# Values spread over a head's partitions: 0/1 products on TensorE, or rows read eight times from HBM

## The chip, the cores and the metric

The kernel runs on one core of a Trainium2 chip. The metric is the device time of one execution in microseconds (us), given as the median of several runs. The core's engines are TensorE (PE, matrix products, with its weight loads listed as PEld), VectorE (DVE), ScalarE (ACT), GpSimd (POOL) and SyncE (SP, which here issues nearly all DMAs). SBUF is the on-chip memory of 128 partitions, PSUM the memory into which TensorE writes its products, HBM the memory off the core.

## The reference

Everything is float32. `x` has 32 batches of 64 tokens of 256 features, and `ctx_2048` the same shape; four blocks follow each other on `x`:

- layer 0: self-attention, cross-attention into `ctx_2048` (16 heads of 16), a GELU MLP;
- layer 1: a recurrent block (32 heads of 8) and a gated feed-forward part;
- layer 2: two cross-attentions (16 heads of 128, with one bias key and value each) and a GELU MLP;
- layer 3: a cross-attention (16 heads of 16) and a GELU MLP.

The change lies in layer 1's recurrence. For each batch and head it keeps an 8×8 state `s`, and for each of the 64 tokens:

```python
def step(s, rkvw):
    r_t, k_t, v_t, w_t = rkvw
    a = k_t[..., :, None] * v_t[..., None, :]
    out = jnp.einsum('bhi,bhij->bhj', r_t, u * a + s)
    s = a + w_t[..., :, None] * s
    return (s, out)
```

So column j of a head's state takes the eight values of k, each times the one value j of v: value j of each head is needed beside all eight of that head's k.

## The kernel before

The 2048 tokens are worked in four groups of 512 (8 batches each, `G`, `GT`, `GB`), and the 256 features lie on partitions in two chunks `c` of 128 (`NC`), so that a chunk holds 16 heads of 8 features. A layer of a group is a Python generator that yields between steps, and `weave(main, lights)` takes steps of the generators in turn at fixed rates:

- layer 0 of group 0, beside `keep`, a filler that makes layer 2's first keys and values (`fk`, `fv`) and stores them in HBM (`kd`, `vd`);
- layer 1 of group 0, beside layer 0 of group 1 and the filler;
- layer 2 of group 0 beside layer 1 of group 1 and layer 0 of group 2; layer 2 of group 1 beside layer 1 of group 2 and layer 0 of group 3; layer 2 of group 2 beside layer 1 of group 3 and layer 3 of group 0;
- then the remaining layers 2 and 3.

So layer 1 of group 0 is the main stream of its stage, while those of groups 1 to 3 are the lighter stream beside the attention of layer 2 (L748 on: products `q2p`, `s2p`, softmax, `pn` on POOL, transposes `tp`, products `pv`, DVE's `o`, then `al_o` through L328). From the order of this program text the scheduler of the framework makes one fixed instruction order per engine; each engine works in order and waits on semaphores.

Tiles come from rotating pools. `banks()` gives one of two double PSUM banks (128×2×512), `bank()` one of four single ones, `big()` one of the 12 SBUF tiles "t4" of 128×2×512. `slot()` loads a 512 KB weight block by a DMA from SP's queue.

In layer 1 (`layer1`, L440), r, k and v of a group are made by `linear` (L165) with the features as partitions, and copied to SBUF by ACT (L521). `ws` holds the decays. `states(c, n)` (L542) makes two of the eight columns j of chunk c's states, n = 0 to 3:

- two products with a 0/1 matrix (L550; columns `C_SEL` of the constants `ct`) take the 32 rows of v that hold value j of the 16 heads, and put each head's row on that head's eight partitions, in the PSUM tile `vj`. The features are laid out so that the 16 rows 16·j to 16·j+15 of a chunk are value j of its 16 heads, and the partitions 8·h to 8·h+7 of the state are head h;
- POOL copies the initial state into column 0 of each batch of `a` (L555);
- DVE multiplies `vj` by k into the remaining columns of `a`, one token later (L559);
- DVE runs the recurrence along the tokens, a scan for each of the two columns (L565);
- POOL multiplies by r (L566).

PE then sums over each head's partitions (`op`, L588). Two states are made ahead; the loop (from L578) makes state n+2 and then consumes state n. After four states of a chunk, `bp` (L595) and two DVE operations on v (L596, L597) complete it, and group norm, gate and output product follow (`gm` L603, `gv` L609).

The helper `beside(i)` raises the priority of the second of two products so that it is placed right behind the first, on other rows of the array.

Of the kernel before, what the change touches and what calls it, by code (L numbers as in the profile page):

```python
# [8 lines left out]
F32 = mybir.dt.float32  # L9
# [5 lines left out]
P = 128  # L15
# [3 lines left out]
GT = NT // G  # L19
GB = B // G  # L20
TT = GT // P
NC = D // P
# [5 lines left out]
C_ID, C_HB, C_HB8, C_SEL, C_GAT, C_M0, C_M1 = 0, 128, 256, 384, 640, 704, 705  # L28
# [40 lines left out]
def kernel(  # L69
# [15 lines left out]
    nc = tc.nc  # L85
    V, A, PL, PE = nc.vector, nc.scalar, nc.gpsimd, nc.tensor
# [4 lines left out]
    sm = ctx.enter_context(tc.tile_pool(name="sm", bufs=2))  # L91
    psum1 = ctx.enter_context(tc.tile_pool(name="ps1", bufs=4, space=bass.MemoryType.PSUM))
    psum2 = ctx.enter_context(tc.tile_pool(name="ps2", bufs=2, space=bass.MemoryType.PSUM))

    def bank(name):
        return psum1.tile([P, 512], F32, tag="b1", name=name)

    def banks(name):
        return psum2.tile([P, 2, 512], F32, tag="b2", name=name)

    def slot(i, pool=lw):
        w = pool.tile([P, WSLOT], F32, tag="w", name=f"w{i}")
        nc.sync.dma_start(w, wts[i])
        return w
# [12 lines left out]
    ct = cp.tile([P, C_N], F32, name="ct")  # L117
# [43 lines left out]
    def linear(ps, w, at, step, y, cols=P):  # L161

        for kc in range(NC):
            o = at + kc * step
            PE.matmul(ps, w[:, o : o + cols], y[:, kc, :], start=(kc == 0), stop=(kc == NC - 1))  # L165
# [251 lines left out]
    @contextmanager  # L417
    def beside(i):

        if i:  # L420
            with tc.high_priority(offset=4000):
                yield
        else:
            yield

    def bt(ap):

        return ap.rearrange("p (b t) -> p b t", b=GB)
# [11 lines left out]
    def layer1(g, work):  # L440
# [3 lines left out]
        def big(name):  # L444
            return work.four(f"{name}_{g}")
# [21 lines left out]
        def mixed(*fs):  # L467

            xms = [big(f"xm{f}") for f in fs]
            parts = [(f, c) for c in range(NC) for f in fs]  # L470
            for two in (parts[:2], parts[2:]):
                if not two:
                    continue
                mp = banks(f"mp_{g}_{two[0][0]}{two[0][1]}")
                for i, (f, c) in enumerate(two):
                    at, rows = c * P, slice(32 * f, 32 * f + 32)
                    if f == 4:
                        at, rows = D + c * P, slice(32 * c, 32 * c + 32)
                    with beside(i):
                        PE.matmul(mp[:, i, :], w6[rows, at : at + P], t5[rows, f // 4, :], start=True, stop=True)  # L480
                for i, (f, c) in enumerate(two):
                    V.scalar_tensor_tensor(
                        xms[fs.index(f)][:, c, :], mp[:, i, :], vec("L1_xattn_maa_stack", 2 * f + c), sx[:, c, :],
                        ALU.add, ALU.mult,
                    )
            for xm in xms:
                PL.tensor_tensor(xm, xm, xa, ALU.add)
            return xms
# [18 lines left out]

        w7 = slot(L1_AT + 2)
        made = {}
        for f, n, at in ((0, "k", 0), (2, "v", 512)):  # L510
            if f == 0:
                xm = xk
            else:
                xm, xr = mixed(2, 3)
                yield
                yield
            made[n] = big(n)
            for c in range(NC):
                ps = bank(f"{n}p1_{g}_{c}")
                linear(ps, w7, at + c * P, D, xm)  # L520
                A.copy(made[n][:, c, :], ps)  # L521
            yield
        w8 = slot(L1_AT + 3)
        xm = xr
# [15 lines left out]
        k, v, r = made["k"], made["v"], made["r"]  # L540

        def states(c, n):  # L542

            j0 = (0, 4, 1, 5)[n]
            vj = banks(f"vj_{g}_{c}_{n}")
            for i in range(2):
                m, q = (j0 + 2 * i) // 2, j0 % 2
                rows = slice(32 * m, 32 * m + 32)
                with beside(i):
                    PE.matmul(  # L550
                        vj[:, i, :], ct[rows, C_SEL + q * P : C_SEL + (q + 1) * P], v[rows, c, :],
                        start=True, stop=True,
                    )
            a = big(f"a{c}{n}")
            PL.tensor_copy(  # L555
                a.rearrange("p i (b t) -> p i b t", b=GB)[:, :, :, 0:1],
                s0t[:, c, j0 : j0 + 3 : 2, g * GB : (g + 1) * GB].unsqueeze(3),
            )
            V.tensor_tensor(  # L559
                a.rearrange("p i (b t) -> p i b t", b=GB)[:, :, :, 1:],  # L560
                vj.rearrange("p i (b t) -> p i b t", b=GB)[:, :, :, :-1],
                bt(k[:, c, :])[:, :, :-1].unsqueeze(1).to_broadcast([P, 2, GB, S - 1]), ALU.mult,
            )
            for i in range(2):
                V.tensor_tensor_scan(a[:, i, :], ws[:, c, :], a[:, i, :], 0.0, ALU.mult, ALU.add)  # L565
            PL.tensor_tensor(a, a, r[:, c : c + 1, :].to_broadcast([P, 2, GT]), ALU.mult)  # L566
            return j0, a

        ruk = big("ruk")
        todo = [(c, n) for c in range(NC) for n in range(4)]  # L570
        ahead = [states(*todo[0])]
        yield
        ahead.append(states(*todo[1]))
        yield
        for c in range(NC):
            V.scalar_tensor_tensor(ruk[:, c, :], r[:, c, :], vec("L1_xattn_u", c), k[:, c, :], ALU.mult, ALU.mult)
        w9 = slot(L1_AT + 4)
        for at, (c, n) in enumerate(todo):  # L578
            if at + 2 < 8:
                ahead.append(states(*todo[at + 2]))  # L580
                yield
            if n == 0:
                op = bank(f"op_{g}_{c}")
            j0, a = ahead.pop(0)
            for i in range(2):
                m, q = (j0 + 2 * i) // 2, j0 % 2
                with beside(i):
                    PE.matmul(  # L588
                        op[32 * m : 32 * m + 32, :], ct[:, C_GAT + 32 * q : C_GAT + 32 * q + 32], a[:, i, :],
                        start=(q == 0), stop=(q == 1),  # L590
                    )
            yield
            if n == 3:
                bp = bank(f"bp_{g}_{c}")
                PE.matmul(bp, hb, ruk[:, c, :], start=True, stop=True)  # L595
                V.tensor_tensor(v[:, c, :], bp, v[:, c, :], ALU.mult)  # L596
                V.tensor_tensor(v[:, c, :], op, v[:, c, :], ALU.add)  # L597
                yield
# [311 lines left out]
            for _ in l[0]:  # L910
                pass

    dp = ctx.enter_context(tc.tile_pool(name="dp", bufs=1, space=bass.MemoryType.DRAM))
    kept = {}

    def keep(pool):
# [156 lines left out]
def build(arrays):  # L1073
    import concourse.bacc as bacc

    nc = bacc.Bacc("TRN2", target_bir_lowering=False, num_devices=1)
    args = [
        nc.dram_tensor(f"in_{n}", a.shape, mybir.dt.from_np(a.dtype), kind="ExternalInput").ap()
        for n, a in arrays.items()
    ]  # L1080
    args.append(nc.dram_tensor("out_0", (P, G, TT, D), F32, kind="ExternalOutput").ap())
    with tile.TileContext(nc) as tc:
        kernel(tc, *args)
    return nc
# [13 lines left out]
```

## Time and profile before

| | |
|---|---|
| runs (us) | 2219.75, 2216.74, 2218.61; median 2218.61 |
| profiled execution (us) | 2216.37, its span 2214.6 |
| granted TensorE clock, mean | 0.97 |
| instructions | 36273 |
| PE busy | 2057.4 us (93%) |
| DVE busy | 1097.3 us (50%) |
| ACT busy | 632.9 us (29%) |
| POOL busy | 597.5 us (27%) |
| DMA, all queues | 197.25 MB, mean 89 GB/s |
| layer 1's states, groups 0 to 3 | about 315 to 400, 583 to 645, 1018 to 1080, 1463 to 1526 us of the span |

The page is taken from one execution; the others can differ by a few tenths of a per cent. Busy time is the time in which an engine executes, not in which it is at its best rate. In a line for a group of instructions stand line, engine, operation, the tile written and the tiles read, the shape and the count, then durations in ns (smallest, median, largest) and first and last start. In a timeline line the bracket at the end gives the idle time before the entry and what released it. A window line gives its length, then the busy time and count of PE, PEld, DVE, ACT and POOL, the granted clock, the busy share of the DMA engines and GB/s.

### The profile page before, as it was taken

The page shows a single profiled execution, that of the slowest core. Times are in us where ns is not written, and L with a number is a line of the kernel's source. Part 1 is how long each engine was busy: PE and PEld are TensorE (multiplying, and loading weights), DVE is VectorE, ACT ScalarE, POOL GpSimd, SP SyncE. Part 2 cuts the span into 40 slices and gives each one's busy share as a digit, 9 for nine tenths or more (in the row PEclk, how much of TensorE's full clock was granted, in tenths as well). Part 3 has the DMA queues.
Part 4 walks back from the last instruction along what each step waited for, and adds up shares of the span by engine and source line. Part 5 has one row for each costly group of instructions (what it writes and reads, how often), then busy time and mean ns, then how long its engine had stood idle before and what let it go on. Part 6 is the DMA issues. An engine that isn't in the chain of part 4 may idle for free. (4 is left out here: it accounts for less than half of the span.)

```text
span 2214.6 us, 36273 instructions
## 1 busy us (share of the span) xinstructions
PE 2057.4 (93%) x15264; PEld 1242.9 (56%) x15264; DVE 1097.3 (50%) x1885; ACT 632.9 (29%) x1000; POOL 597.5 (27%) x498
## 2 busy tenths in 40 slices
PE   5889998899999898999997999999999999999998
PEld 3445444354555465755554656555566767565665
DVE  3552557423655636335556463266564355424661
ACT  1222322132321322232313132322233233222442
POOL 2331344213423314214324141233221112200220
PEclk9999998999999999999998999999999999999999
DMA  7233231226412212243121123341213342213010
GB/s 247 93 106 118 93 110 57 93 101 229 141 49 64 66 41 63 92 132 109 55 62 58 42 79 96 121 134 44 86 45 108 100 152 69 78 51 94 22 41 20
DMA packets 79794, 197.25 MB, mean 89 GB/s; under 512 B 9616, under 2 KB 14352, under 8 KB 79632
## 3 DMA queue, kind: packets, MB, share of 16 engines
q1 hardware_dynamic: 77472, 191.88, 27.1%
q8 instruction: 121, 1.98, 0.4%
q0 software_dynamic: 576, 2.10, 0.3%
q10 hardware_dynamic: 1584, 0.95, 0.2%
q14 instruction: 41, 0.34, 0.1%
HBM read 158.98 MB, written 35.91 MB: 88 GB/s over the span
## 5 line engine op out<-in xcount | busy, mean ns | idle before, releaser
L165 PE MATMUL q2p<-h,w 128*128 128x512 f32 x512 | 245.4, 612 | 6.8 <-DMA w<-in_wts 3.2
L328 PE MATMUL al_o<-w,o 128*128 128x256 f32 x1024 | 235.1, 388 | 11.7 <-DVE o L828 10.7
L328 PEld LDWEIGHTS al_o<-w,o 128*128 128x128 f32 x1024 | 196.6, 194 | 52.6 <-issue 20.6
L778 ACT ACTIVATE q<-q2p,vt 128x512 f32<-128x512 f32 x128 | 87.5, 685 | 278.9 <-PE q2p L165 275.7
L165 PEld LDWEIGHTS q2p<-h,w 128*128 128x128 f32 x512 | 94.9, 193 | 123.6 <-issue 105.5
L796 POOL TENSOR_TENSOR pn<-s,sm 128x512 f32<-128x512 f32 x64 | 69.7, 1091 | 285.2 <-DVE sm L209 198.2
L165 PE MATMUL k2p_f<-c,w 128*128 128x512 f32 x256 | 131.2, 634 | 4.9 <-DMA w<-in_wts 2.8
L726 PE MATMUL v2p_f<-w,c 128*128 128x512 f32 x256 | 122.4, 601 | 0.0
L165 PE MATMUL k2p<-c,w 128*128 128x512 f32 x256 | 120.7, 597 | 0.0
L726 PE MATMUL v2p<-w,c 128*128 128x512 f32 x256 | 119.1, 609 | 1.1 <-DVE k L764 1.1
L566 POOL TENSOR_TENSOR a<-a,r 128x1024 f32<-128x1024 f32 x32 | 76.1, 2378 | 109.8 <-DVE a L565 96.4
L937 DVE TENSOR_TENSOR fv<-v2p_f,vb 128x512 f32<-128x512 f32 x64 | 43.9, 687 | 124.7 <-PE v2p_f L726 124.7
L928 ACT ACTIVATE fk<-k2p_f,vt 128x512 f32<-128x512 f32 x64 | 43.9, 686 | 175.4 <-PE k2p_f L165 146.8
L341 DVE TENSOR_TENSOR x<-al_o,x 128x512 f32<-128x512 f32 x64 | 43.6, 683 | 101.2 <-PE al_o L328 101.2
L828 DVE TENSOR_SCALAR o<-pv,vt 128x256 f32<-128x256 f32 x128 | 55.8, 473 | 76.6 <-PE pv L817 76.4
L764 DVE TENSOR_SCALAR k<-k2p,vt 128x512 f32<-128x512 f32 x64 | 47.4, 743 | 91.4 <-PE k2p L165 91.4
L788 PEld LDWEIGHTS s2p<-k,q 128*64 128x64 f32 x2048 | 67.7, 138 | 40.8 <-issue 29.7
L817 PEld LDWEIGHTS pv<-pt,v 64*64 64x64 f32 x4096 | 72.8, 140 | 26.6 <-issue 18.4
L565 DVE TENSOR_TENSOR_SCAN a<-ws,a 128x512 f32<-128x512 f32 x64 | 85.4, 1368 | 1.7
L726 PEld LDWEIGHTS v2p_f<-w,c 128*128 128x128 f32 x256 | 49.6, 195 | 63.5 <-issue 61.3
L817 PE MATMUL pv<-pt,v 64*64 64x64 f32 x4096 | 81.7, 226 | 3.2 <-issue 1.5
L165 PEld LDWEIGHTS k2p<-c,w 128*128 128x128 f32 x256 | 49.4, 193 | 62.1 <-issue 59.4
(305 smaller groups left out, 3678.5 us busy)
## 6 DMA issues: line engine op xcount, KB each, us to landing
w<-in_wts SPq DMA_DIRECT2D x200, 512.0 KB, 3.7
kd<-fk SPq DMA_DIRECT2D x64, 260.0 KB, 2.1
k<-kd SPq DMA_DIRECT2D x64, 260.0 KB, 3.8
vd<-fv SPq DMA_DIRECT2D x64, 256.0 KB, 2.0
v<-vd SPq DMA_DIRECT2D x64, 256.0 KB, 4.5
vb<-in_vrow SPq DMA_DIRECT2D x20, 256.0 KB, 4.1
vs<-in_vrow SPq DMA_DIRECT2D x20, 256.0 KB, 3.4
c<-in_cT POOLq DMA_DIRECT2D x4, 512.0 KB, 11.6
```

Of the source, the lines that this page charges most:

```text
L165: PE.matmul(ps, w[:, o : o + cols], y[:, kc, :], start=(kc == 0), stop=(kc == NC - 1))
L328: PE.matmul(ps[:, a, :], y[kc][:, i * P : (i + 1) * P], wk[:, o : o + D], start=(kc == 0), stop=(kc == k - 1),)
L565: V.tensor_tensor_scan(a[:, i, :], ws[:, c, :], a[:, i, :], 0.0, ALU.mult, ALU.add)
L566: PL.tensor_tensor(a, a, r[:, c : c + 1, :].to_broadcast([P, 2, GT]), ALU.mult)
L726: PE.matmul(ps, cs[g][:, kc, bp * P : (bp + 1) * P], wv[:, 512 * kc : 512 * kc + 512], start=(kc == 0), stop=(kc == NC - 1),)
L764: V.tensor_scalar_add(k[:, :, :S], bt(ps), vec(f"L2_xattn_bk{a}", hd))
L778: A.activation(q, ps, AF.Identity, bias=vec(f"L2_xattn_bq{a}", hd))
L788: PE.matmul(sp[64 * h2 : 64 * h2 + 64, b // 4, (b % 4) * (S + 1) : (b % 4 + 1) * (S + 1)], qs[h2][:, b * S : (b + 1) * S], ks[h2][:, b, :] ...
L796: PL.tensor_tensor(pn, s[:, :, :S], rc.unsqueeze(2).to_broadcast([P, GB, S]), ALU.mult)
L817: PE.matmul(pv[b2][rows, to : to + S], vals[bp][half, hc : hc + 64], pt[half, bp, h2 * S : (h2 + 1) * S], start=True, stop=True,)
L828: V.tensor_scalar_add(ov[:, :, 1, :], src[1], bv)
L928: A.activation(k[:, :, :S], bt(ps), AF.Identity, bias=vec("L2_xattn_bk1", hd))
```

## The change

The two products of a state are left out, and with them the PSUM tile `vj`. Each chunk of v is stored to HBM as it is made (256 KB, `spread`). For each of a state's two columns a DMA then reads the column's 16 rows back, each eight times, and writes them to the 128 partitions of `a`, shifted by one token (255.5 KB). DVE's multiply reads `a` and writes it in place. The pool `dp` of HBM tensors is opened earlier, so that layer 1 can use it.

```diff
+    dp = ctx.enter_context(tc.tile_pool(name="dp", bufs=1, space=bass.MemoryType.DRAM))
...
         made = {}
+        spread = [dp.tile([P, GT], F32, name=f"vs{g}{c}", tag=f"vs{g}{c}") for c in range(NC)]
...
                 A.copy(made[n][:, c, :], ps)
+                if n == "v":
+                    nc.sync.dma_start(spread[c], made[n][:, c, :])
...
             j0 = (0, 4, 1, 5)[n]
-            vj = banks(f"vj_{g}_{c}_{n}")
+            a = big(f"a{c}{n}")
             for i in range(2):
-                m, q = (j0 + 2 * i) // 2, j0 % 2
-                rows = slice(32 * m, 32 * m + 32)
-                with beside(i):
-                    PE.matmul(
-                        vj[:, i, :], ct[rows, C_SEL + q * P : C_SEL + (q + 1) * P], v[rows, c, :],
-                        start=True, stop=True,
-                    )
-            a = big(f"a{c}{n}")
+                j = j0 + 2 * i
+                nc.sync.dma_start(
+                    a[:, i, 1:],
+                    spread[c][16 * j : 16 * j + 16, : GT - 1].unsqueeze(1).to_broadcast([16, 8, GT - 1]),
+                )
             PL.tensor_copy(
                 a.rearrange("p i (b t) -> p i b t", b=GB)[:, :, :, 0:1],
                 s0t[:, c, j0 : j0 + 3 : 2, g * GB : (g + 1) * GB].unsqueeze(3),
             )
             V.tensor_tensor(
                 a.rearrange("p i (b t) -> p i b t", b=GB)[:, :, :, 1:],
-                vj.rearrange("p i (b t) -> p i b t", b=GB)[:, :, :, :-1],
+                a.rearrange("p i (b t) -> p i b t", b=GB)[:, :, :, 1:],
                 bt(k[:, c, :])[:, :, :-1].unsqueeze(1).to_broadcast([P, 2, GB, S - 1]), ALU.mult,
             )
...
-    dp = ctx.enter_context(tc.tile_pool(name="dp", bufs=1, space=bass.MemoryType.DRAM))
     kept = {}
```

## The prediction

> **What bounds the kernel now.** I read the page's engine totals first, then the tile that the change removes, stage by stage, then the orders of PE, DVE and POOL around it, then the transfers.
>
> The totals:
>
> ```profile
> PE 2057.4 (93%) x15264; PEld 1242.9 (56%) x15264; DVE 1097.3 (50%) x1885; ACT 632.9 (29%) x1000; POOL 597.5 (27%) x498
> q1 hardware_dynamic: 77472, 191.88, 27.1%
> ```
>
> TensorE (PE) is busy for 93% of the span, and the DMA engines are idle for some 70%. So work taken off PE can shorten the kernel, but only where PE isn't waiting anyway. The removed tile `vj`, then PE's busy time on it in the four stages that hold it (groups 0 to 3), and last the same stages for the whole core (PE, PEld, DVE, ACT, POOL busy, then clock, DMA share, GB/s):
>
> ```profile
> L550 PE MATMUL vj<-v,ct x128: 587/692/1217, 316.4 to 1509.2; 32*128 32x512 f32 x128
> L559 DVE TENSOR_TENSOR a<-vj,k x32: 1177/1198/1209, 317.5 to 1509.9; 128x1008 f32<-128x1008 f32 x32
> 315.00:400.00 85.00, 9.97 (x32) 2.60 (x32) 9.50 (x8) 0.88 0.18 64
> 583.00:645.00 62.00, 7.90 (x32) 2.11 (x32) 9.57 (x8) 0.93 0.31 95
> 1018.00:1080.00 62.00, 7.90 (x32) 2.11 (x32) 9.58 (x8) 0.94 0.30 94
> 1463.00:1526.00 63.00, 8.18 (x32) 2.38 (x32) 9.59 (x8) 1.00 0.30 93
> 315.00:400.00 85.00, 69.08 (x377) 32.95 (x376) 67.36 (x71) 19.29 (x32) 41.96 (x28) 0.88 0.18 64
> 583.00:645.00 62.00, 54.96 (x481) 31.04 (x483) 42.68 (x49) 12.82 (x21) 25.12 (x15) 0.93 0.31 95
> 1463.00:1526.00 63.00, 60.92 (x690) 33.74 (x692) 46.68 (x58) 16.40 (x29) 25.79 (x16) 1.00 0.30 93
> ```
>
> The products cost PE 9.97 + 7.90 + 7.90 + 8.18 = 33.95 us, 1.06 us per tile of two (32 tiles). That is the ceiling, but for idle that goes with them. Group 0's stage is no PE stage: PE 69.1 of 85 us, DVE 67.4. Groups 1 and 2 leave PE idle for 7 of 62; group 3 for 2 of 63. What the products stand beside, group 1 then group 3 (start, length, idle before and its releaser):
>
> ```profile
> 596.81 1.13 PE L550 MATMUL vj<-v,ct 32*128 32x512 f32 x4
> 599.88 1.05 PE L588 MATMUL op<-a,ct 128*32 128x512 f32 x4 [0.84 <-POOL a L566]
> 602.89 1.10 PE L328 MATMUL al_o<-w,o 128*128 128x256 f32 x4 [0.90 <-PE vj L550]
> 607.17 8.57 PE L328 MATMUL al_o<-w,o 128*128 128x256 f32 x28 [3.18 <-DVE o L828]
> 641.52 1.05 PE L588 MATMUL op<-a,ct 128*32 128x512 f32 x4 [2.11 <-POOL a L566]
> ...
> 1469.67 6.28 PE L328 MATMUL al_o<-w,o 128*128 128x256 f32 x28 [0.72 <-DVE o L828]
> ```
>
> The 28 `al_o` products take 6.28 us in group 3 and 8.57 in group 1 behind the 3.18 us idle: an idle PE costs its length and about 2.3 us of slow clock.
>
> **What is removed.** 64 products (128 matmul and 128 weight-load rows), and DVE's wait for them.
>
> Group 0: 9.97 us leave PE, but DVE fills 79% of the stage and PE has its own waits there, the longest of 5.47 us for a DVE `fv` (L937) at 395.31, behind the last two scans (386.92, 7.75 us). In the changed order those scans come earlier, as chunk 1's third and fourth states do. Half of 9.97 is taken, 5, less the wait for `y_b` below, 2, plus 2 of the late idle: −5 (bounds −9 and +4).
>
> Groups 1 and 2, each: in the first half three tiles (3.2) come off a busy PE; the others stood in front of waits for the same DVE and POOL chain, but that chain no longer waits for PE (0.84 and 0.90 were such waits) and begins up to 3.6 us earlier, as the second multiply on `vj` moves ahead: −3.5 together. The three later tiles (620.28, 627.90, 631.02) stand among busy PE work: −3.2. The wait of 2.11 at 641.52 for POOL ends earlier, with the slow clock behind it: −2.3. With 1 back for DVE, below: −8 (bounds −10 and −4).
>
> Group 3: the first three tiles end just ahead of the wait for `o`. DVE, not PE, sets its end, and in the changed order one multiply (1.2 us) stands ahead of `o`, so these 3.2 us become idle. The five later ones give 5.3; 2.3 goes back if that idle turns the clock down. −3 (bounds −5.3 and +1).
>
> **What is added.** On SP's queue, 8 stores of 256 KB and 64 loads of 255.5 KB (128 rows of 2044 B), 72 DMAs and 18.8 MB on 197. The nearest rows, the last a row read 128 times:
>
> ```profile
> vd<-fv SPq DMA_DIRECT2D x64, 256.0 KB, 2.0
> v<-vd SPq DMA_DIRECT2D x64, 256.0 KB, 4.5
> vs<-in_vrow SPq DMA_DIRECT2D x20, 256.0 KB, 3.4
> 530.00:546.00 16.00, 12.21 (x57) 5.22 (x58) 5.34 (x9) 5.93 (x8) 2.07 (x2) 0.89 0.97 339
> ```
>
> A load lands in 3.4 to 4.5 us; I take 4, since the source is a tensor just written, as for `vd`. At 339 GB/s, which a full stretch reached, 18.8 MB are 55 us of transfer, in stages that use 18 to 31% of the DMA engines. The store's 2.0 is hidden: `r` and the gate's products come between it and the first state. Costed at nothing on SP: at the 0.32 to 0.43 us that it takes for an issue it has 23 to 31 us more to do, over 2215; its place in order matters more. In group 1 the loads stand behind a weight load that waits for `q2p` (578.5), so the first lands at about 583, before 584.33 where the first product stood. The fourth state's loads wait there for the first state's `op`, and eight `v` loads queue behind them, issued near 601 and not from 593; they are needed at 643, so 8 us of delay are covered by 40.
>
> Two waits are new. POOL's copy of column 0 (L555) now waits for the landing, since it writes the tile that the DMA fills, and all later POOL work is queued behind it in order. In group 0 the second state's copy stands behind an add that ends at 317.33; the scans on DVE then wait for it, and `y_b` (318.67) behind them starts some 2 us later, with PE's `qp_b` waiting. In group 1 the copy for the fifth state stands ahead of a `pn` multiply due at 592.54: a weight load and ten loads (3.07 MB) have 13.6 us to land, so 226 GB/s decides. In group 3 it is 2.05 MB in 9.5 us, 216 GB/s. At 339 both are covered.
>
> DVE's multiply (L559) now reads both inputs from SBUF. `L205`, two SBUF inputs of the same size, and the scan (also two):
>
> ```profile
> L205 DVE TENSOR_TENSOR s_b<-s_b,mx_b x16: 1182/1216/2756, 124.6 to 1299.4; 128x1024 f32<-128x1024 f32 x16
> L565 DVE TENSOR_TENSOR_SCAN a<-ws,a x64: 1160/1214/3294, 319.4 to 1512.7; 128x512 f32<-128x512 f32 x64
> ```
>
> Both have the median of L559 but a long tail that it lacks (their means are 1336 and 1368): +0.14 to 0.17 each, 4.5 to 5.5 us of DVE in all; no bound for PE but in group 0 and at the two waits for `o`, and counted there with 1 per stage.
>
> [...]
>
> **Sum.** −5 − 8 − 8 − 3 = −24 on the profiled execution's 2216.37 (span 2214.6 and 1.77 around it), 2.24 below the median of the runs. Against 2218.61: 2194.6, so 2195.
>
> **Rivals.** (1) *The products stood in waits.* DVE and POOL set these stages, PE idles where it worked, and each such idle turns the clock down. Group 0 even, groups 1 and 2 at −4, group 3 at +1: −7, so 2211 (2206 to 2217). For it: the 3.18 and 5.47 waits. Against it: in groups 1 to 3 at least five tiles of eight stand among busy PE rows.
>
> (2) *The loads land late and POOL is held* (slower). Below about 220 GB/s in the burst the column-0 copies hold POOL's in-order queue: `pn` and the L566 products slip, then `tp` and `op` on PE. Landing twice as late, 8 us and not 4, is 6 to 8 us per stage and 2 of slow clock; four stages cost 32 to 40, against 24 gained: +8 to +16. The fourth state's second load, queued behind eight `v` loads in groups 1 and 2, can add some 2 each, so +14: 2232 (2222 to 2245). It decides from a landing of about 7 us on, where the 24 are eaten up. For it: rows shorter than 2 KB, eight reads of each row, and the slowest row, 4.5, is the one just written. Against it: 339 GB/s in the full stretch.
>
> That the change doesn't do what it says is excluded: in the program as built, the products are gone and all 72 DMAs are there.
>
> **Numbers.** 0.2%, or 4.4 us, is about what a measurement of this kernel can tell from no change. Forecast 0.53 (own range 2184 to 2206), rival 1 0.22, rival 2 0.25. Faster: 0.53 and the 0.12 of rival 1 below 2214; same: its 0.09 and 0.01 of rival 2; slower: 0.24 and 0.01. The range 2181 to 2230 leaves out some 0.13 of rival 2 and 0.04 below.
>
> **What would show it.** Right: L550 gone and PE's busy time near 2025; the loads of `a` landing in 3.4 to 4.5 us; the stages of groups 1 and 2 some 8 us shorter than 62, group 3's by 3; the multiply's mean at 1.34 to 1.37. Wrong: PE waiting for POOL's `pn` or `a` behind a copy that a DMA released (rival 2), or PE's busy time down by 34 with the stages as long and the clock lower (rival 1). Forecast and rival 1 part at −12 us.

## The result, and the profile after

The changed kernel takes 2233.82 us (median of four runs, 2230.9 to 2237.07) against 2218.12: a ratio of 1.0071 (95% interval 1.0053 to 1.0088). The forecast was 2195, the range 2181 to 2230. So 24 us were expected to go, and 15.7 were added. The profiled execution took 2233.39 us, its span 2231.6, 17.0 more than before's 2214.6. Each ratio here and below is against the kernel before as it ran beside that kernel.

The totals, the costs of what layer 1's states do (busy us, mean ns, idle before), and the loads' landing (KB each, median us from issue to arrival):

```profile
PE 2042.6 (92%) x15136; PEld 1246.0 (56%) x15136; DVE 1134.2 (51%) x1885; ACT 632.9 (28%) x1000; POOL 630.6 (28%) x498
L567 DVE TENSOR_TENSOR_SCAN a<-ws,a 128x512 f32<-128x512 f32 x64 | 100.0, 1599 | 0.4
L568 POOL TENSOR_TENSOR a<-a,r 128x1024 f32<-128x1024 f32 x32 | 85.8, 2683 | 58.1 <-DVE a L567 57.9 <-POOL a L557 0.2
L561 DVE TENSOR_TENSOR a<-a,k 128x1008 f32<-128x1008 f32 x32 | 61.5, 1941 | 7.2 <-DMA a<-vs 7.2
L557 POOL COPY a<-s0t 128x16 f32<-128x16 f32 x32 | 30.6, 969 | 31.4 <-DMA a<-vs 31.4
a<-vs SPq DMA_DIRECT2D x64, 255.5 KB, 6.3
```

The first three of these before:

```profile
L565 DVE TENSOR_TENSOR_SCAN a<-ws,a 128x512 f32<-128x512 f32 x64 | 85.4, 1368 | 1.7
L566 POOL TENSOR_TENSOR a<-a,r 128x1024 f32<-128x1024 f32 x32 | 76.1, 2378 | 109.8 <-DVE a L565 96.4 <-DVE sm L209 13.3
L559 DVE TENSOR_TENSOR a<-vj,k 128x1008 f32<-128x1008 f32 x32 | 38.2, 1198 | 14.3 <-PE vj L550 14.0
```

No instruction was added on DVE or POOL, yet DVE is busy for 37 us more and POOL for 33. The scans took 14.6 us more and the multiply 23.3, which is all of DVE's part; POOL's product took 9.7 more and its copy of column 0 20.8 (9.8 before), 30.5 of POOL's 33. PE's busy time fell by 15 and not by 34. What is left ran at a lower mean granted clock, 0.961 against 0.970, and an estimate that takes busy time as inverse to the clock accounts for it: 2057.4 less 34 is 2023.4, and times 0.970/0.961, 2042. The stages of groups 0, 1 and 3, in the columns shown for before:

```profile
315.00:400.00 85.00, 63.49 (x345) 32.43 (x344) 74.08 (x71) 19.43 (x32) 53.67 (x34) 0.84 0.34 107
583.00:645.00 62.00, 50.24 (x427) 29.87 (x426) 54.52 (x53) 12.47 (x21) 33.01 (x21) 0.92 0.48 140
1463.00:1526.00 63.00, 44.35 (x494) 25.10 (x493) 52.27 (x50) 14.52 (x26) 35.14 (x20) 0.89 0.55 152
```

Group 3's stage went from 97% busy PE to 44.35 of 63 us. PE's waits for `pn` in groups 1 and 3 (group 2's is 3.65 us), and last the longest that it had before, in group 3 (idle and releaser at the end):

```profile
593.88 0.66 PE L804 MATMUL tp<-ct,pn 128*128 128x128 f32 x4 [3.70 <-POOL pn L798]
1510.14 1.12 PE L804 MATMUL tp<-ct,pn 128*128 128x128 f32 x4 [11.88 <-POOL pn L798]
1500.27 0.66 PE L802 MATMUL tp<-ct,pn 128*128 128x128 f32 x4 [1.02 <-POOL pn L796]
```

What DVE and POOL did ahead of the wait of 11.88 us, and last two entries of DVE before, from the same place:

```profile
1487.43 4.45 DVE L561 TENSOR_TENSOR a<-a,k 128x1008 f32<-128x1008 f32 x2
1491.81 6.66 DVE L567 TENSOR_TENSOR_SCAN a<-ws,a 128x512 f32<-128x512 f32 x4
1498.39 0.67 DVE L202 TENSOR_REDUCE mx<-s2p 128x8 f32<-128x520 f32 x1
1498.98 3.03 DVE L561 TENSOR_TENSOR a<-a,k 128x1008 f32<-128x1008 f32 x1
...
1487.66 3.16 POOL L568 TENSOR_TENSOR a<-a,r 128x1024 f32<-128x1024 f32 x1 [2.34 <-DVE a L567]
1498.61 2.34 POOL L568 TENSOR_TENSOR a<-a,r 128x1024 f32<-128x1024 f32 x1 [1.23 <-DVE a L567]
1505.02 3.15 POOL L568 TENSOR_TENSOR a<-a,r 128x1024 f32<-128x1024 f32 x1 [2.93 <-DVE a L567]
1508.14 1.95 POOL L798 TENSOR_TENSOR pn<-s,sm 128x512 f32<-128x512 f32 x1
...
1483.40 0.69 DVE L200 TENSOR_REDUCE mx<-s2p 128x8 f32<-128x520 f32 x1
...
1489.58 1.20 DVE L559 TENSOR_TENSOR a<-vj,k 128x1008 f32<-128x1008 f32 x1
```

Two multiplies take 4.45 us in place of 2.4. The second began at 1488.54, while POOL's product ran, and ended at 1491.88, 1.07 us after that product. In the trace 13 of the 32 multiplies are long (3.01 us on average; the other 19 take 1.21), and each of the 13 began while a POOL instruction with SBUF inputs ran and ended 1.06 or 1.07 us after it. So did two more that met the end of a `pn` multiply and took 1.40 us. Before, with `vj` as one input, 13 of the 32 multiplies began during a POOL instruction, 0.45 us or more ahead of its end, and none of them took more than 1.21 us. In these two traces that reads as a lock on the multiply with two SBUF inputs: it waits for POOL's whole instruction, then runs.

A second thing is to be seen: the multiplies and scans of chunk 1's first two states now stand ahead of the softmax's first reduction (`mx`, L202). Before, `mx` (L200, at 1483.40) stood behind chunk 0's last multiply, ahead of chunk 1's first (1489.58).

### The profile page after: what moved, and what is told of

Its sections match the earlier page's. It is cut to its first block, busy times and chain, and to the rows that moved or that the text cites. A ratio compares the mean times of both kernels' runs of the same rounds, so it can differ in the third digit from the quotient of the medians.

```text
span 2231.6 us, 36185 instructions
## 1 busy us (share of the span) xinstructions
PE 2042.6 (92%) x15136; PEld 1246.0 (56%) x15136; DVE 1134.2 (51%) x1885; ACT 632.9 (28%) x1000; POOL 630.6 (28%) x498
## 5 line engine op out<-in xcount | busy, mean ns | idle before, releaser
L568 POOL TENSOR_TENSOR a<-a,r 128x1024 f32<-128x1024 f32 x32 | 85.8, 2683 | 58.1 <-DVE a L567 57.9
L567 DVE TENSOR_TENSOR_SCAN a<-ws,a 128x512 f32<-128x512 f32 x64 | 100.0, 1599 | 0.4
L790 PE MATMUL s2p<-k,q 128*64 128x65 f32 x2048 | 79.7, 227 | 10.2 <-ACT q L780 6.8
L202 DVE TENSOR_REDUCE mx<-s2p 128x8 f32<-128x520 f32 x64 | 44.4, 694 | 85.1 <-PE s2p L790 85.0
## 6 DMA issues: line engine op xcount, KB each, us to landing
a<-vs SPq DMA_DIRECT2D x64, 255.5 KB, 6.3
```

Source lines behind the costliest of these rows:

```text
L202: V.tensor_reduce(mx, src, AX.X, ALU.max)
L790: PE.matmul(sp[64 * h2 : 64 * h2 + 64, b // 4, (b % 4) * (S + 1) : (b % 4 + 1) * (S + 1)], qs[h2][:, b * S : (b + 1) * S], ks[h2][:, b, :] ...
```

## The experiments

Three theories, each of which could hold the loss:

- **A, landing**: the loads land in 6.3 us and not 4; POOL's copies wait for them in order, and what is behind them is late.
- **B, port** (a name alone: the traces show who waits for whom, not by what in the chip): a DVE instruction with two SBUF inputs and a POOL instruction that reads SBUF shut each other out for whole instructions, as in the 13 long multiplies. The products' tile in PSUM kept the multiply out of that (1.21 us at most).
- **C, order**: with nothing from PE to wait for, DVE's order has states ahead of the softmax.

### Without the DMAs: no_loads

```diff
-                if n == "v":
-                    nc.sync.dma_start(spread[c], made[n][:, c, :])
...
-            for i in range(2):
-                j = j0 + 2 * i
-                nc.sync.dma_start(
...
-                a.rearrange("p i (b t) -> p i b t", b=GB)[:, :, :, 1:],
+                bt(v[:, c, :])[:, :, :-1].unsqueeze(1).to_broadcast([P, 2, GB, S - 1]),
```

> The changed kernel without its 72 DMAs: no store of v, no load, and the multiply reads the unspread v from SBUF (so the spread itself is left out). Theory A (landing: loads that land in 6.3 us hold POOL's copies and all behind them): the time falls below the kernel before, to about 2195 (-24), because products and loads are both gone. Theory B (port: a multiply with two SBUF inputs and POOL's reads of SBUF shut each other out, multiply 1198 to 1941 ns): most of the loss stays, 2222 to 2232, with the multiply's mean still above 1.6 us. Theory C (order: nothing paces the multiplies any more, so DVE does states ahead of the softmax's reductions): also 2222 to 2232, with PE still waiting 8 us or more for pn in group 3.

Measured: 2224.77 us, ratio 1.0034 (1.0023 to 1.0045). With neither products nor DMAs the kernel is still slower than before. The group of the multiply, then PE's wait for `pn` in group 3:

```profile
L553 DVE TENSOR_TENSOR a<-v,k 128x1008 f32<-128x1008 f32 x32 | 54.5, 1730 | 0.0
1504.96 1.12 PE L796 MATMUL tp<-ct,pn 128*128 128x128 f32 x4 [9.65 <-POOL pn L790]
```

A falls as the main cause: some 8 us (0.37%, from two ratios that are uncertain by 0.1 to 0.2%) lie between this kernel and the changed one. B and C stay.

### The port alone, with before's order: port_only, copies_only, both_sbuf

port_only, on the kernel before (copies_only has the first line alone; both_sbuf has the exchange of the input alone):

```diff
+            V.tensor_copy(a[:, :, 1:2], vj[:, :, 0:1])
             V.tensor_tensor(
                 a.rearrange("p i (b t) -> p i b t", b=GB)[:, :, :, 1:],
-                vj.rearrange("p i (b t) -> p i b t", b=GB)[:, :, :, :-1],
+                bt(v[:, c, :])[:, :, :-1].unsqueeze(1).to_broadcast([P, 2, GB, S - 1]),
```

The expectations for port_only, copies_only and both_sbuf, in this order:

> As both_sbuf, but DVE first copies two elements per partition out of the products' tile into the multiply's output tile, so that the multiply keeps its place and its wait for PE as in the kernel before (32 small copies of about 0.1 us are added; the spread is left out of the result). B: slower by 8 to 20 (2226 to 2238), the multiply's mean at 1.6 to 1.9 us and not 1.2. A and C: within 5 of before, 2214 to 2223, with the multiply under 1.4 us.

> The kernel before with only the 32 two-element copies of port_only added (0.15 us each there, 4.8 us of DVE in all); the multiply reads the products' tile in PSUM as before. If port_only's +24 us is the port's (theory B): this one within 6 of before, multiply at 1.20 us. If it is the small copies' and the waits they bring: +15 or more here too, and B loses its best witness.

> The kernel before with its products, but the multiply reads the unspread v from SBUF, so nobody waits for the products (the spread is left out of the result). No DMA is added. A: no slower than before, 2212 to 2220. B and C both: slower than before by 10 to 25, since port and free order are there and the products' 34 us as well: 2228 to 2243. Its distance to no_loads is what the products are worth on PE once DVE no longer waits for them: 24 by the prediction.

Measured: port_only 2240.89 us, 1.0108 (1.0083 to 1.0133); copies_only 2221.07, 1.0007 (0.9992 to 1.0021); both_sbuf 2262.32, 1.0203 (1.0182 to 1.0223). The multiply in port_only, then in copies_only:

```profile
L560 DVE TENSOR_TENSOR a<-v,k 128x1008 f32<-128x1008 f32 x32 | 53.7, 1677 | 1.0
L560 DVE TENSOR_TENSOR a<-vj,k 128x1008 f32<-128x1008 f32 x32 | 38.5, 1204 | 0.9
```

The orders of these two differ in a few places of group 0 alone, and the products' tile comes free before port_only's multiply and not behind it. Otherwise nothing but where one input lies differs, and it costs 1.0% of the time, 22 us: B. With the order free as well (both_sbuf) it is 21 us more; both losses are larger than expected, port_only's by 3 us and both_sbuf's by 19. both_sbuf and no_loads differ by the products: 37.6 us, not the 24 of the expectation, and a little over the 34 of their busy time.

### Pacing by buffers: a3

```diff
-            a = big(f"a{c}{n}")
+            a = work.pool.tile([P, 2, 512], F32, tag="a4", name=f"a{c}{n}_{g}", bufs=3)
...
-        wka = Work(work_stack.enter_context(tc.tile_pool(name="wa", bufs=T4_BUFS)))
+        wka = Work(work_stack.enter_context(tc.tile_pool(name="wa", bufs=9)))
```

> The changed kernel with a pool of three tiles for the states of layer 1 (and nine others in place of twelve), so that the load of state n+3 waits for PE to have consumed state n, and DVE's order has the softmax's reductions between the states again. C: 10 or more of the 15.7 us come back, 2215 to 2224, and group 3's wait for pn goes from 11.9 to under 4. B: the multiply stays near 1.9 us and the time within 5 of 2234. A: slower still, 2238 to 2250, since each load now starts later and its landing is waited for.

Measured: 2231.59 us, 1.0065 (1.0041 to 1.0089), the multiply at 1600 ns. PE's longest wait for `pn` in group 3 fell from 11.88 to 2.62 us and the stage's loss from 12.0 to 3.8, as C has it, but DVE waited 40.1 us for landings (7.2 in the changed kernel) and groups 1 and 2 lost 7.1 and 7.6 (the section on why the prediction was wrong says how the stages are measured). Of C's expectation the wait came true and the time didn't. The run is inconclusive for C, since it changed the loads' times along with the order: what order gave, later loads may have taken.

### Without POOL's product: before_nor, after_nor

In both kernels:

```diff
-            PL.tensor_tensor(a, a, r[:, c : c + 1, :].to_broadcast([P, 2, GT]), ALU.mult)
```

> The kernel before without POOL's product by r (so r is left out of the states' output); a baseline for after_nor. All theories: a little faster than before, 2200 to 2216, since PE's waits for that product (5.9 us and 8.7 of its weight loads) go.

> The changed kernel without POOL's product by r. The DMAs, the free order and the two SBUF inputs stay; what goes is the 2.35 us read that shuts the multiply and the scans out. B: 15 to 30 faster than before_nor (about 2180 to 2195), the multiply at 1.2 to 1.4 us, the scans at 1.2 to 1.3. A: no faster than before_nor by more than 8, POOL still waiting 30 us for landings and DVE too. C: PE still waits 8 us or more for pn in group 3, no faster than before_nor by more than 8.

Measured: before_nor 2202.02 us, 0.9922 (0.99 to 0.9945); after_nor 2181.71, 0.984 (0.982 to 0.986). Multiply and scans of after_nor:

```profile
L561 DVE TENSOR_TENSOR a<-a,k 128x1008 f32<-128x1008 f32 x32 | 38.4, 1220 | 4.8 <-DMA a<-vs 4.8
L567 DVE TENSOR_TENSOR_SCAN a<-ws,a 128x512 f32<-128x512 f32 x64 | 75.3, 1215 | 0.5
```

With POOL's product gone the change makes the kernel 20.3 us shorter, not 15.7 longer, although its loads land late (a median of 6.8 us) and DVE has the same free order in group 3, where PE's wait for `pn` is now 3.80 us. So neither A nor C does the harm by itself. It needs the meeting with POOL's product.

### One input through PSUM: act_psum

On the changed kernel:

```diff
+            vj = banks(f"vj_{g}_{c}_{n}")
+            A.copy(vj[:, :, 1:], a[:, :, 1:])
             PL.tensor_copy(
...
-                a.rearrange("p i (b t) -> p i b t", b=GB)[:, :, :, 1:],
+                vj.rearrange("p i (b t) -> p i b t", b=GB)[:, :, :, 1:],
```

> The changed kernel, but ACT copies the landed rows into a PSUM tile (32 copies of 128x1022, about 1.1 us each by the 128x1024 ACT rows, 35 us of an engine that is 28% busy), and the multiply reads that tile and k, so that it has one SBUF input as in the kernel before. The full result is computed. B: 2195 to 2212, multiply at 1.20 us. A: 2228 or more, since the landing is waited for as before and the copy comes on top. C alone can't be told from B here, since the copies also pace the multiplies.

Measured: 2189.73 us, 0.9874 (0.9854 to 0.9895): 27.6 us faster than before and some 43 faster than the changed kernel, for 32 more instructions on ACT. Its totals, the multiply, and ACT's copy:

```profile
PE 2026.6 (93%) x15136; PEld 1237.0 (57%) x15136; DVE 1102.8 (50%) x1885; ACT 663.3 (30%) x1032; POOL 601.1 (27%) x498
L563 DVE TENSOR_TENSOR a<-vj,k 128x1008 f32<-128x1008 f32 x32 | 37.5, 1189 | 8.7 <-ACT vj L558 8.7
L558 ACT COPY vj<-a 128x1022 f32<-128x1022 f32 x32 | 32.4, 1014 | 33.8 <-DVE a L563 20.5 <-DMA a<-vs 6.4 <-DVE s_b L387 4.5
```

PE is busy for 31 us less than before, DVE and POOL are back within 6 us of where they were, and no multiply is longer than 1209 ns, though 23 of the 32 began while a POOL instruction ran. The landings are the same 6.3 us. The time is 5 us below what was expected of B. By itself this run doesn't part B from C, since ACT's copies also pace the multiplies; port_only and after_nor do.

### What the landings cost: landr, act_rows, act_noload

landr takes the changed kernel, act_rows takes act_psum; in each the rows land in a tile of their own:

```diff
+            rows = big(f"rows{c}{n}")
...
-                    a[:, i, 1:],
+                    rows[:, i, 1:],
```

(landr loads whole rows, unshifted, and the multiply takes the shift.) act_noload is act_psum without stores and loads, its ACT copy reading v.

The expectations for landr, act_psum run again, act_rows and act_noload, in this order:

> The changed kernel, but the rows land in a tile of their own, and the multiply goes from there to the state's tile, so that POOL's copy of column 0 no longer waits for a landing (the copies waited 31 us in the changed kernel). Full result. B (port): the multiply still has two SBUF inputs, 1.7 to 1.95 us, and no more than 6 of the 15.7 us come back (2226 to 2234). A (landing, by way of POOL's copies): 12 or more come back, 2222 or less.

> act_psum again, beside the next two on one chip: 2186 to 2194.

> act_psum, but the rows land in a tile of their own and the state's tile is taken only for the multiply, so POOL's copies of column 0 wait for nothing (they waited 40 us for ACT's copies in act_psum). Full result. B: POOL is off the path by now, so 2183 to 2192, at most 5 faster than act_psum. If the copies held POOL's products: 2180 or less.

> act_psum without its 72 DMAs: ACT copies the unspread v into the PSUM tile (the spread is left out of the result). The distance to act_psum is what the landings of 6.3 us and the traffic still cost once the port is cured: by no_loads against the changed kernel it was 9 us there, so 2181 or so; if the landings are covered now, 2186 to 2190.

Measured on one chip: landr 2230.89 us, 1.0057 (1.0043 to 1.0072); act_psum again 2191.07, 0.9873 (0.9857 to 0.9889); act_rows 2186.89, 0.9858 (0.9846 to 0.9871); act_noload 2189.79, 0.988 (0.9866 to 0.9894). landr's multiply and its landings:

```profile
L562 DVE TENSOR_TENSOR a<-rows,k 128x1008 f32<-128x1008 f32 x32 | 58.2, 1835 | 4.5 <-DMA rows<-vs 4.5
rows<-vs SPq DMA_DIRECT2D x64, 256.0 KB, 4.7
```

Freeing POOL's copies from the landings gave back 3 of the 15.7 us, within the two intervals' overlap. And with one input of the multiply in PSUM, leaving out all 72 DMAs gives nothing (act_noload 2189.79 against act_psum's 2191.07). So the landings, late as they are, cost no time that these runs can tell where the multiply has one SBUF input. act_rows has the lowest median of the kernels that compute the whole result; its lead over act_psum lies within their intervals.

## Why the prediction was wrong

By stage, in us against before. Each figure is how much later the same PE products start in the kernel's trace than in before's, taken at 304, 425, 575, 684, 1006, 1135, 1440 and 1545 us of before's span. Single figures scatter by 1 to 3 us (copies_only: −2.0 to +3.2).

| | group 0 | group 1 | group 2 | group 3 | sum |
|---|---|---|---|---|---|
| forecast | −5 | −8 | −8 | −3 | −24 |
| changed kernel | −2.1 | +0.6 | +3.5 | +12.0 | +14.0 |
| port_only | +0.9 | +4.0 | +6.1 | +6.6 | +17.6 |
| act_psum | −11.1 | −6.9 | −8.0 | −0.2 | −26.2 |

- **What is removed: right in sum, in part by luck.** With the multiply's input in PSUM (act_psum) the four stages gave −26.2, where −24 was forecast. Groups 1 and 2 were met within 1.1, but group 0 gave 6.1 us more than forecast and group 3 2.8 less, and these two cancel in part. PE's busy time came to 2026.6 there, near the 2025 named; in the changed kernel it was 2042.6.
- **DVE's multiply with two SBUF inputs: the step that failed.** It put +0.14 to 0.17 us on each, 4.5 to 5.5 in all, from the means of two other operations of that kind; of the 1 us per stage that it names for this, its sums hold it in groups 1 and 2 alone. Measured: +0.74 on each, 23.3 in all, and it passed the loss on: scans +14.6, POOL's product +9.7, POOL's copies +20.8. The price of such a meeting could be read from before's trace: 2 of the 16 `L205` operations shown and 12 of the 64 scans took over 1.4 us (up to 2756 and 3294 ns), and each ended 1.08 or 1.09 us after the POOL instruction that it met, as each of the changed kernel's long multiplies ended 1.06 or 1.07 us after one. What could not be carried over was how often it happens: `L205` seldom met POOL's work, while this multiply follows in DVE's order right behind the scans that release POOL's product. 15 of 32 met a POOL instruction, 13 of them for long. port_only and after_nor show it from both sides: two SBUF inputs alone cost 22 us, and without POOL's product the change gains 20.
- **The parts of the loss, along one path through the runs.** From before to port_only +24 us (some 2 of it the small copies), to both_sbuf +21 (free order under the lock), to no_loads −38 (the products), to the changed kernel +8 (the DMAs): +15.7. Along another path the parts differ: with one input in PSUM the DMAs cost nothing that shows.
- **Landing: the duration was wrong and cost little.** 4 us were taken, 6.3 measured. POOL did wait, 31.4 us, with its copies of column 0, as rival 2 has it. But rival 2, whose number (2232) and side came out, gave the wrong cause: neither the DMAs' absence (no_loads) nor freeing POOL's copies (landr) brings the time back to before's, and act_psum has the same landings.
- **Group 0's wait for `y_b`** was foreseen at 2 us and became 5.17 of idle for `qp_b`. The first multiply there took 3.08 us and ended 1.07 after POOL's add: again the lock, and not the landing.
- **Order.** That DVE would take later states earlier was seen, and counted as a gain in groups 0 to 2. The free order shows no loss where POOL's product is left out (after_nor has it and gains 20), but under the lock it goes with 21 us more (both_sbuf against port_only). In no_loads PE's longest wait in group 3 is then for `pn` (9.65 us), in both_sbuf for `o` (4.86 us). Which part of the changed kernel's 11.88 us wait is order and which is length isn't settled: the wait is 2.62 with another order in a3, but a3 moved the loads too, and 3.80 with the same order in after_nor, which also freed POOL.

## What to carry to other kernels

Before an elementwise operand is moved from PSUM to SBUF, see what GpSimd does at that moment. Here the multiply kept its median (1208 ns, 1198 before), but 13 of 32 were held until a GpSimd instruction had ended, and both engines lost: DVE was busy for 37 us more, GpSimd for 33. Count the meetings from the two engines' orders around that instruction, not from the mean of a like operation elsewhere. Where ACT has room (it was busy for 28% here), a copy of one operand into PSUM can be worth its price: at 1.01 us each, 32 of them turned +15.7 into −27.6 us, with the pacing that the copies bring included.

## What the runs showed of the hardware

- The multiply with one input in PSUM was not shut out: 13 of 32 in before and 23 of 32 in act_psum began while a POOL instruction ran, and none took more than 1209 ns.
- POOL was shut out too: its copy of column 0 (128x16) went from a mean of 346 ns to 969, and its product from 2378 to 2683. In the changed kernel 25 of the 32 copies took over 1 us, and each of these ended 0.00 to 0.07 us after a DVE multiply or scan. Of the 32 products 13 took 3.11 to 3.32 us and the others 2.34 to 2.37, and each of the 13 began 0.22 to 0.30 us behind the start of a DVE multiply or scan.
- The scan, with two SBUF inputs, was in it as well: its mean was 1368 ns before and 1599 in the changed kernel, where 17 of 64 took over 1.4 us (12 before) and each of these ended 1.08 or 1.09 us after a POOL instruction. Once POOL's product was left out it was 1221 (before_nor) and 1215 (after_nor), so a part of before's scan time was this already.
- 64 loads that read each row eight times landed in 6.3 us in the changed kernel and in act_psum, but in 4.7 in landr, with whole rows of 2048 bytes into another tile. Neither row length nor tile is needed for the short landing: the changed kernel's own loads, issued at other times in a3, landed in 4.4 us, and 2044-byte rows into a tile of their own (act_rows) in 5.2. That points to the time of issue, which no run varied alone.
